# A selective-scan layer with attention beside it: products moved a step later, two engines in source order

## The chip, the cores and the metric

The kernel runs on one core of a Trainium2 chip. The metric is the device time of one execution in microseconds (us); the median of three runs of the kernel before is 5548.85 us (5548.56 to 5548.85). TensorE does the matrix products into PSUM, VectorE and ScalarE do the elementwise work, the scans and the activations, GpSimd a few copies and the indirect transfers, and SyncE (SP) issues nearly all DMAs. Each engine works through its own queue in order; semaphores tie the queues together.

## The reference, cut to what matters

One decoder layer on x of shape (8, 512, 512): a Mamba block, cross-attention with 16 heads over a context of 512 rows, and a mixture of 32 experts with a gate and a shared expert; a layer norm stands after each.

```python
# the Mamba block: D_INNER = 1024, D_STATE = 16
xn = layernorm(x);  x_main, z = split(xn @ in_proj_w)
x_main = silu(causal_depthwise_conv(x_main))          # 4 taps
dt, B_ssm, C_ssm = split(x_main @ x_proj_w)
dt = softplus(dt @ dt_proj_w + dt_proj_b)
# for every time step t, channel d, state n:
h = exp(A * dt) * h + dt * B_ssm * x_main
y = sum_n(h * C_ssm) + x_main * D_param
out = res_scale * ((y * silu(z)) @ out_proj_w) + residual
# then
x = layernorm(x + out)
x = layernorm(x + cross_attention(x, ctx))
x = layernorm(x + experts(x))
```

## The kernel before

All data are float32. The function `layers` holds the Mamba block, the attention, the gate and the shared expert; `experts` and `finish` come after it. The span has three parts: the scan loop up to about 3700 us, the attention of the last batch alone up to about 3945 us, and the experts and the last layer norm.

**The scan loop.** The eight batches are cut into chunks of T = 256 time steps, two per batch (t = 0 and 1), so 16 chunks. A chunk has 32 steps k, one for each pair of channel blocks q (4), group of four states g (4) and channel block ci (2); 512 steps in all. A step scans four states of 128 channels at once. Its pieces:

- `carry` (L448): takes a buffer h (four exist) and ScalarE copies the state from the chunk before into its column 0 (L452).
- `decays` (L442): ScalarE computes exp(A·dt) into one of two buffers l_da, four activations (L446). It is called one step ahead, for step k+1.
- `scan` (L455): VectorE multiplies dt·x by the broadcast B (L458), runs the scan over 1028 columns (L462) and, in a first chunk, saves the state (L464).
- `collect` (L466): VectorE multiplies h by the broadcast C (L479); TensorE adds the states up into the PSUM tile py with four products by a constant matrix (L483), and for g = 0 puts D·x under them with two more (L471).
- `gated` (L491): after eight steps VectorE multiplies the gate z by py (L495). There is one py.
- `bcast` (L380): DMAs that spread B and C of the next group over the partitions, six buffers bc.

**Work beside the scans.** At fixed steps the loop also calls `back` (the output projection of the chunk before, L512, and its layer norm), `gate_x` (z, L311 and L357), `prepare` (softplus of dt for the next q: L398 on TensorE, L408 to L414 on ScalarE, L418 to L421 on VectorE, then the DMAs into `both`), `norm_x`, `flip_x`, `convolve` (L311, L331, L337 and the taps L345) and `x_proj` for the next chunk. A list `side` holds the attention, gate and shared expert of the batch before, cut into units with a weight: `maximum` (L775 on TensorE, L777 on VectorE), `weigh` (L801, exponential L805 on ScalarE), `gather` (L817), dense products (L712) and others. The function `work` gives the weight of each step's own TensorE work, and units are taken as long as the weights keep pace.

**How consumers are placed.** A unit returns a closure that holds the work of the next engine. `do` runs a unit, then lets every closure that is waiting take one stage (`settle`), then appends the new one; `dry` runs `settle` until nothing is left.

**What sets the order.** Every engine's queue is made by the scheduler: it plays the program through with a cost model and issues what is ready, by priority. Source order is only the priority, except for the instructions pinned with `keep_in_program_order`. PSUM tiles that are shared: two of tag mm (dense products, projections), two of tag sc (ps_s and ps_t), one py, one po.

Of the kernel before, what the change touches and what calls it, by code (L numbers as in the profile page):

```python
# [8 lines left out]
F32 = mybir.dt.float32  # L9
# [3 lines left out]
ALU = mybir.AluOpType  # L13
# [4 lines left out]
P = 128  # L18
# [6 lines left out]
NST = 16  # L25
RANK = 32
CC = DI // P
T = 256
NT_ = T // P
NG = 4  # L30
HP = P // 2
# [51 lines left out]
def layers(ctx, tc, a, x1d, filld, based, xbuf):  # L83
# [23 lines left out]
    nc = tc.nc  # L107
# [11 lines left out]
    psy = ctx.enter_context(tc.tile_pool(name="l_psy", bufs=1, space=PSUM))  # L119
# [322 lines left out]
    def decays(c, g, dt, da):  # L442

        for n in range(NG):
            j, m = n // 2, n % 2
            nc.scalar.activation(da[:, n, 1:], dt[:, c % 2, j, :], AF.Exp, scale=aneg[:, c, j, g, m : m + 1])  # L446

    def carry(t, c, g):  # L448

        last = state[:, c, g].unsqueeze(2)  # L450
        h = mp.tile([P, NG, T + 1], F32, tag="h", name="h", bufs=4)
        nc.scalar.copy(h[:, :, 0:1], last if t else nothing)  # L452
        return h
# [9 lines left out]
        if t < S // T - 1:  # L463
            nc.vector.tensor_copy(state[:, c, g].unsqueeze(2), h[:, :, T : T + 1])  # L464

    def collect(c, g, h, bc, py, f):  # L466


        if g == 0:
            for j in range(2):  # L470
                nc.tensor.matmul(  # L471
                    py[j * HP : (j + 1) * HP, c % 2, :],
                    ident[:, j * HP : (j + 1) * HP],
                    f["xs"][c // 2][:, c % 2, :],
                    start=(c % 2 == 0),
                    stop=False,
                )
        steps = h.rearrange("p (j m) t -> p j m t", j=2)[:, :, :, 1:]
        nc.vector.tensor_tensor(steps, steps, bc[1], ALU.mult)  # L479
        for m in range(NG // 2):  # L480
            for j in range(2):
                s = (g, m, c % 2)
                nc.tensor.matmul(  # L483
                    py[j * HP : (j + 1) * HP, c % 2, :],
                    twice,
                    h[:, j * 2 + m, 1:],
                    start=False,
                    stop=(s == (NST // NG - 1, NG // 2 - 1, 1)),
                )

    def gated(q, f, py):  # L491

        f["xs"].pop(q)
        pair = f["zs"][:, 2 * q : 2 * q + 2, :]
        nc.vector.tensor_tensor(pair, pair, py, ALU.mult)  # L495
# [518 lines left out]
    def do(fn, *args, first=False):  # L1014

        if first:
            dry()
        rest = fn(*args)
        settle()
        if rest:  # L1020
            left.append(rest)

    def work(k):

        front = 6.9 if k in (1, 2) else 3.4 if 3 <= k < 7 or k in (12, 15, 18, 21, 24) else 1.0 if k in (11, 26) else 0.0
        return 1.2 + front

    f = {"xt": x0}
# [12 lines left out]
    bc, n = bcast(f, 0), 0  # L1041
    nc.scalar.activation(aneg, aneg, AF.Exp)
    nc.vector.tensor_scalar(aneg, aneg, -1.0, None, ALU.mult)
    decays(0, 0, f["ready", 0][0], das[0])
    old, side, cleared = None, [], 0

    for i, (b, t) in enumerate(chunks):
        nf = {}
        after = chunks[i + 1] if i + 1 < len(chunks) else None
        if t == 0:  # L1050
            side, spent = units(b - 1) if b else sources(0), 0.0

            own = [work(k) for k in range(len(steps))] * 2
            whole = sum(own) + sum(x[0] for x in side)
        py = None
        for k, (q, g, ci) in enumerate(steps):
            if ci == 0:
                if (q, g) != (CC // 2 - 1, NST // NG - 1):
                    bcn = bcast(f, (g + 1) % (NST // NG))
                else:  # L1060
                    bcn = bcast(nf, 0) if after else None
            h = carry(t, 2 * q + ci, g)

            if k + 1 < len(steps) or after:
                nq, ng, ni = steps[(k + 1) % len(steps)]
                decays(2 * nq + ni, ng, (f if k + 1 < len(steps) else nf)["ready", nq][0], das[(n + 1) % 2])
            scan(t, 2 * q + ci, g, f["ready", q][1], bc, das[n % 2], h)
            n += 1
            if k % 8 == 0:
                if k:  # L1070
                    gated(q - 1, f, py)
                elif old:
                    gated(CC // 2 - 1, old[2], old[3])
                py = psy.tile([P, 2, T], F32, tag="py", name="py")
            if i == 0 and k == 0:
                load("Wo")
            if i == 0 and k == 2:
                biases()
            if k == 0 and old:
                twice_x(*old[:3])  # L1080
# [12 lines left out]
            if after:  # L1093
                if k == 5:
                    load_x(*after, nf)
                if k == 9:
                    norm_x(nf)
                if k == 11:
                    for j in range(DC // 2):
                        do(flip_x, j, nf)  # L1100
                if k in (12, 15, 18, 21):
                    do(convolve, after[1], (k - 12) // 3, nf, first=(k == 12))
                if k == 23:
                    dry()
# [19 lines left out]
        old = (b, t, f, py)  # L1124
        f = nf
    gated(CC // 2 - 1, old[2], old[3])
    twice_x(*old[:3])
    for j in range(2):
        do(back, j, *old[:3], first=True)
    dry()  # L1130
    for _, fn, alone in units(B - 1):
        do(fn, first=alone)
# [347 lines left out]
```

## Time and profile before

| | us |
|---|---|
| median of three runs | 5548.85 |
| the profiled execution | 5555.79 |
| its span, first to last instruction | 5554.1 |
| TensorE busy | 4883.9 |
| VectorE busy | 4349.2 |
| ScalarE busy | 2592.8 |
| scans L462: 512 of 2291 ns | 1169.4 |
| products with B and C, L458 and L479 | 617.5 and 621.9 |
| decays L446: 2048 of 499 ns | 888.7 |

The page is one execution on the chip. Busy time of TensorE is modelled: matmuls are pipelined, and the tail of each group counts. "Idle before" is time in which an engine stood still ahead of an instruction, put down to the engine that ended it. Forty equal slices of the span, in tenths of busy time, show that VectorE is nearly full for two thirds of the span and TensorE in the rest:

```profile
PE   6768889888988988888888898879899999999994
DVE  7998989989889989899989999864466565555554
ACT  5554565655556555555555655523222222222223
```

### The profile page before, as it was taken

The page shows a single profiled execution, that of the slowest core. Times are in us where ns is not written, and L with a number is a line of the kernel's source. Part 1 is how long each engine was busy: PE and PEld are TensorE (multiplying, and loading weights), DVE is VectorE, ACT ScalarE, POOL GpSimd, SP SyncE. Part 2 cuts the span into 40 slices and gives each one's busy share as a digit, 9 for nine tenths or more (in the row PEclk, how much of TensorE's full clock was granted, in tenths as well). Part 3 has the DMA queues.
Part 4 walks back from the last instruction along what each step waited for, and adds up shares of the span by engine and source line. Part 5 has one row for each costly group of instructions (what it writes and reads, how often), then busy time and mean ns, then how long its engine had stood idle before and what let it go on. Part 6 is the DMA issues. An engine that isn't in the chain of part 4 may idle for free. (4 is left out here: it accounts for less than half of the span.)

```text
span 5554.1 us, 60352 instructions
## 1 busy us (share of the span) xinstructions
PE 4883.9 (88%) x19752; PEld 2720.5 (49%) x19752; DVE 4349.2 (78%) x5738; ACT 2592.8 (47%) x5483; POOL 560.9 (10%) x424
## 2 busy tenths in 40 slices
PE   6768889888988988888888898879899999999994
PEld 3334344334434434443443343333577777777773
DVE  7998989989889989899989999864466565555554
ACT  5554565655556555555555655523222222222223
POOL 1000002002000200200010020010111111111111
PEclk7878999999999999999999999989999999999997
DMA  6887345445534634544463464441345444454444
GB/s 183 246 239 203 108 130 184 114 120 154 167 104 113 203 92 129 184 123 113 124 199 104 114 193 110 113 157 44 102 121 125 125 125 124 121 126 124 115 121 146
DMA packets 554282, 769.83 MB, mean 139 GB/s; under 512 B 135754, under 2 KB 268394, under 8 KB 551920
## 3 DMA queue, kind: packets, MB, share of 16 engines
q1 hardware_dynamic: 517952, 677.55, 41.5%
q0 software_dynamic: 33280, 76.90, 7.3%
q10 hardware_dynamic: 2736, 11.54, 0.5%
q8 instruction: 156, 2.56, 0.2%
q14 instruction: 158, 1.29, 0.1%
HBM read 508.68 MB, written 165.05 MB: 121 GB/s over the span
## 5 line engine op out<-in xcount | busy, mean ns | idle before, releaser
L446 ACT ACTIVATE l_da<-both,l_aneg 128x256 f32<-128x256 f32 x2048 | 888.7, 499 | 791.5 <-DVE h L462 744.2
L462 DVE TENSOR_TENSOR_SCAN h<-l_da,h 128x1028 f32<-128x1028 f32 x512 | 1169.4, 2291 | 49.9 <-ACT h L452 27.3
L483 PE MATMUL py<-h,l_twice 128*64 128x256 f32 x4096 | 632.0, 424 | 194.2 <-DVE h L479 194.0
L458 DVE TENSOR_TENSOR h<-both,bc 128x1024 f32<-128x1024 f32 x512 | 617.5, 1213 | 141.8 <-PE py L483 78.2
L479 DVE TENSOR_TENSOR h<-h,bc 128x1024 f32<-128x1024 f32 x512 | 621.9, 1218 | 6.3 <-DMA l_qa<-l_ka 0.3
L483 PEld LDWEIGHTS py<-h,l_twice 128*64 128x64 f32 x4096 | 295.2, 148 | 570.5 <-issue 246.4
L775 PE MATMUL ps_s<-l_ka,l_qa 64*128 64x512 f32 x1024 | 315.2, 695 | 141.9 <-DVE mx L777 141.4
L1230 PE MATMUL ps_h<-xT,w 128*128 128x320 f32 x1536 | 435.6, 433 | 0.0
L1310 POOL DMA_INDIRECT based<-y,xe x160 | 251.2, 1570 | 1313.4 <-ACT y L1333 573.4
L1251 DVE TENSOR_TENSOR hT<-ps_h,p 128x320 f32<-128x320 f32 x128 | 62.9, 491 | 379.1 <-PE ps_h L1230 379.1
L777 DVE TENSOR_REDUCE mx<-ps_s 128x2 f32<-128x1024 f32 x256 | 310.2, 1215 | 56.2 <-PE ps_s L775 55.5
L1230 PEld LDWEIGHTS ps_h<-xT,w 128*128 128x128 f32 x1536 | 292.2, 190 | 118.2 <-issue 0.4
L801 PE MATMUL ps_t<-l_qa,l_ka 64*128 64x512 f32 x1024 | 300.6, 651 | 15.0 <-ACT eT L805 11.4
L805 ACT ACTIVATE eT<-ps_t 128x1024 f32<-128x1024 f32 x256 | 258.7, 1012 | 109.2 <-PE ps_t L801 108.7
L817 PE MATMUL po<-eT,l_va 128*64 128x512 f32 x1024 | 281.5, 628 | 24.6 <-ACT raw L829 20.8
L650 POOL DMA_INDIRECT xbuf<-x2t,dest x128 | 218.7, 1708 | 815.8 <-DVE dest L644 777.4
L1230 PE MATMUL ps_h<-t,s 128*128 128x320 f32 x1024 | 286.1, 432 | 0.0
L712 PE MATMUL ps_p<-x2T,wa 128*128 128x512 f32 x512 | 247.5, 633 | 11.8 <-DVE hT L892 10.3
L311 PE MATMUL ps_z<-xnT,wm 128*128 128x256 f32 x1024 | 241.0, 389 | 17.8 <-DVE o L521 17.0
L311 PE MATMUL ps_x<-xnT,wm 128*128 128x256 f32 x1024 | 242.5, 390 | 2.9 <-DMA wm<-in_in_proj_w 2.0
L512 PE MATMUL po<-wm,zs 128*128 128x512 f32 x512 | 234.6, 608 | 3.9 <-DMA wm<-in_out_proj_w 1.8
L1230 PEld LDWEIGHTS ps_h<-t,s 128*128 128x128 f32 x1024 | 194.6, 190 | 81.1
(234 smaller groups left out, 7414.6 us busy)
## 6 DMA issues: line engine op xcount, KB each, us to landing
bc<-scr SPq DMA_DIRECT2D x1024, 128.0 KB
w<-in_w SPq DMA_DIRECT2D x93, 1024.0 KB
wm<-in_in_proj_w SPq DMA_DIRECT2D x128, 512.0 KB
xbuf<-zero SPq DMA_DIRECT2D x32, 1362.5 KB
xe<-xbuf SPq DMA_DIRECT2D x32, 1362.5 KB
both<-dt SPq DMA_DIRECT2D x256, 128.0 KB
both<-dtx SPq DMA_DIRECT2D x256, 128.0 KB
wm<-in_out_proj_w SPq DMA_DIRECT2D x64, 512.0 KB
```

What stands on the lines that cost most here:

```text
L311: nc.tensor.matmul(ps[:, i, :], w[:, dc, i * P : (i + 1) * P], f["xnT"][:, dc, :], start=(dc == 0), stop=(dc == DC - 1),)
L446: nc.scalar.activation(da[:, n, 1:], dt[:, c % 2, j, :], AF.Exp, scale=aneg[:, c, j, g, m : m + 1])
L458: nc.vector.tensor_tensor(steps, dtx[:, c % 2].unsqueeze(2).to_broadcast([P, 2, NG // 2, T]), bc[0], ALU.mult)
L462: nc.vector.tensor_tensor_scan(flat, da.rearrange("p n t -> p (n t)"), flat, 0.0, ALU.mult, ALU.add)
L479: nc.vector.tensor_tensor(steps, steps, bc[1], ALU.mult)
L483: nc.tensor.matmul(py[j * HP : (j + 1) * HP, c % 2, :], twice, h[:, j * 2 + m, 1:], start=False, stop=(s == (NST // NG - 1, NG // 2 - 1, 1)),)
L775: nc.tensor.matmul(ps[:, j, :], qa[r, lt * P : (lt + 1) * P], ka[r, :], start=True, stop=True)
L777: return lambda: nc.vector.tensor_reduce(mx[:, lt, :].unsqueeze(2), ps, AX.X, ALU.max) and None
L801: nc.tensor.matmul(ps[:, j, :], ka[r, kc * P : (kc + 1) * P], qa[r, :], start=True, stop=True)
L805: nc.scalar.activation(eT, ps, AF.Exp)
L817: nc.tensor.matmul(po[j * 2 * HD : (j + 1) * 2 * HD, :], va[:, kc, i, j * HD : (j + 2) * HD], eT[:, j, :], start=(kc == 0), stop=(kc == SC ...
L1230: nc.tensor.matmul(ps, w[:, n, r * P : (r + 1) * P], x[:, n, :], start=not more and n == 0, stop=n == 1, skip_group_check=more,)
```

## The change

Four things change, all in `layers` and its call:

1. `collect` keeps the product with C on VectorE, but returns its TensorE products as a closure, which the loop calls at the end of the next step, ahead of that step's own `collect`. py is now taken inside that closure and kept in `f`; `gated` moves from steps 0, 8, 16, 24 to 1, 9, 17, 25.
2. `carry` is called one step ahead, beside `decays`.
3. `settle` is called right behind the scan, and again only by the units of the step; the call ahead of `collect` is gone. `back`, `gate_x` and silu of z come one step later (2 and 3, 4 to 7, 8), and `work` and the condition for side units follow them.
4. The scheduler no longer orders TensorE and VectorE inside `layers`: both take the source's order. ScalarE, GpSimd and SP are still ordered by the scheduler, with the other two given.

```diff
-    def collect(c, g, h, bc, py, f):
-        if g == 0:
-            for j in range(2):
-                nc.tensor.matmul(
-                    py[j * HP : (j + 1) * HP, c % 2, :],
-                    ident[:, j * HP : (j + 1) * HP],
-                    f["xs"][c // 2][:, c % 2, :],
-                    start=(c % 2 == 0),
-                    stop=False,
-                )
+    def collect(c, g, h, bc, f):
         steps = h.rearrange("p (j m) t -> p j m t", j=2)[:, :, :, 1:]
         nc.vector.tensor_tensor(steps, steps, bc[1], ALU.mult)
-        for m in range(NG // 2):
...
+        xs = f["xs"][c // 2]
+        def products():
+            if g == 0 and c % 2 == 0:
+                f["py"] = psy.tile([P, 2, T], F32, tag="py", name="py")
+            py = f["py"]
+            if g == 0:
...
+            for m in range(NG // 2):
...
+        return products
-    def gated(q, f, py):
+    def gated(q, f):
...
-        front = 6.9 if k in (1, 2) else 3.4 if 3 <= k < 7 or k in (12, 15, 18, 21, 24) else 1.0 if k in (11, 26) else 0.0
+        front = 6.9 if k in (2, 3) else 3.4 if 4 <= k < 8 or k in (12, 15, 18, 21, 24) else 1.0 if k in (11, 26) else 0.0
...
+    ahead, products = carry(0, 0, 0), None
...
-            h = carry(t, 2 * q + ci, g)
+            h = ahead
             if k + 1 < len(steps) or after:
                 nq, ng, ni = steps[(k + 1) % len(steps)]
+                ahead = carry(t if k + 1 < len(steps) else after[1], 2 * nq + ni, ng)
                 decays(...)
             scan(t, 2 * q + ci, g, f["ready", q][1], bc, das[n % 2], h)
-            if k % 8 == 0:
-                if k:
-                    gated(q - 1, f, py)
+            if k % 8 == 1:
+                if k > 1:
+                    gated(q - 1, f)
                 elif old:
-                    gated(CC // 2 - 1, old[2], old[3])
-                py = psy.tile([P, 2, T], F32, tag="py", name="py")
+                    gated(CC // 2 - 1, old[2])
...
-            if k in (1, 2) and old:
-                do(back, k - 1, *old[:3], first=True)
-            if 3 <= k < 7:
-                do(gate_x, k - 3, f, first=(k == 3))
-            if k == 7:
+            settle()
+            if k in (2, 3) and old:
+                do(back, k - 2, *old, first=True)
+            if 4 <= k < 8:
+                do(gate_x, k - 4, f, first=(k == 4))
+            if k == 8:
                 dry()
                 silu(f["zs"])
...
-            if side and (k >= 3 or t and k == 0):
+            if side and (k >= 4 or t and k < 2):
...
-            settle()
-            collect(2 * q + ci, g, h, bc, py, f)
+            if products:
+                products()
+            products = collect(2 * q + ci, g, h, bc, f)
...
+    products()
+    gated(CC // 2 - 1, old[2])
...
         with ExitStack() as ctx:
+            ctx.enter_context(tc.manual_schedule(engines={mybir.EngineType.DVE, mybir.EngineType.PE}))
             layers(ctx, tc, a, x1d, filld, based, xbuf)
```

More of the change, by code (lines that the diff above doesn't have):

```diff
@@ L464, in scan @@
             nc.vector.tensor_copy(state[:, c, g].unsqueeze(2), h[:, :, T : T + 1])
-    def collect(c, g, h, bc, py, f):
-        if g == 0:
-            for j in range(2):
-                nc.tensor.matmul(
-                    py[j * HP : (j + 1) * HP, c % 2, :],
-                    ident[:, j * HP : (j + 1) * HP],
-                    f["xs"][c // 2][:, c % 2, :],
-                    start=(c % 2 == 0),
-                    stop=False,
-                )
+    def collect(c, g, h, bc, f):
         steps = h.rearrange("p (j m) t -> p j m t", j=2)[:, :, :, 1:]
         nc.vector.tensor_tensor(steps, steps, bc[1], ALU.mult)
-        for m in range(NG // 2):
[L481 to L489, printed above, removed]
-    def gated(q, f, py):
+        xs = f["xs"][c // 2]
[4 more added lines that the diff above has]
+            if g == 0:
+                for j in range(2):
+                    nc.tensor.matmul(
+                        py[j * HP : (j + 1) * HP, c % 2, :],
+                        ident[:, j * HP : (j + 1) * HP],
+                        xs[:, c % 2, :],
+                        start=(c % 2 == 0),
+                        stop=False,
+                    )
+            for m in range(NG // 2):
+                for j in range(2):
+                    s = (g, m, c % 2)
+                    nc.tensor.matmul(
+                        py[j * HP : (j + 1) * HP, c % 2, :],
+                        twice,
+                        h[:, j * 2 + m, 1:],
+                        start=False,
+                        stop=(s == (NST // NG - 1, NG // 2 - 1, 1)),
+                    )
+        return products
+    def gated(q, f):
         f["xs"].pop(q)
         pair = f["zs"][:, 2 * q : 2 * q + 2, :]
-        nc.vector.tensor_tensor(pair, pair, py, ALU.mult)
+        nc.vector.tensor_tensor(pair, pair, f["py"], ALU.mult)
     def twice_x(b, t, f):
@@ L1054, in layers @@
             whole = sum(own) + sum(x[0] for x in side)
-        py = None
         for k, (q, g, ci) in enumerate(steps):
@@ L1079, in layers @@
             if k == 0 and old:
-                twice_x(*old[:3])
-            if k in (1, 2) and old:
-                do(back, k - 1, *old[:3], first=True)
-            if 3 <= k < 7:
-                do(gate_x, k - 3, f, first=(k == 3))
-            if k == 7:
+                twice_x(*old)
+            settle()
[4 more added lines that the diff above has]
+            if k == 8:
                 dry()
@@ L1123, in layers @@
             do(fn, first=alone)
-        old = (b, t, f, py)
+        old = (b, t, f)
         f = nf
-    gated(CC // 2 - 1, old[2], old[3])
-    twice_x(*old[:3])
+    products()
+    gated(CC // 2 - 1, old[2])
+    twice_x(*old)
     for j in range(2):
-        do(back, j, *old[:3], first=True)
+        do(back, j, *old, first=True)
     dry()
```

## The prediction

> **What bounds the kernel now.** I read the windows view first, to see which engine has no room, then the waits of that engine, then its timeline, to see what a wait and a step without a wait cost. Three stretches: the scan loop with everything beside it (70 to 3700 us), the last batch's attention alone (to 3945), the experts (to 5554).
>
> ```profile
> 70.00:3700.00 3630.00, 3093.65 (x12640) 1472.95 (x12640) 3293.36 (x3782) 2039.82 (x4346) 272.76 (x197) 0.92 0.51 147
> 3945.00:5554.00 1609.00, 1535.90 (x6272) 1133.85 (x6270) 925.95 (x1724) 452.68 (x978) 251.22 (x160) 0.98 0.48 122
> ```
>
> The columns are the stretch, its length, busy us of TensorE, its weight load, VectorE, ScalarE and GpSimd, then clock, DMA share and GB/s. In the scan loop VectorE is busy 3293 of 3630 us; only 337 us are left to win there. TensorE's 3094 us are less than they look: eight records of py last 1.08 us as a group, but the next group starts 0.92 us after them (2009.17 to 2010.09), so the tail of each group is counted as busy. The experts are TensorE's and lie outside the changed functions. So the question is what VectorE waits for in the loop, before and after. Its waits between 70 and 3700 us, the longest:
>
> ```profile
> DVE h L458 <- PE py L483: 78.2, 33, 5.2
> DVE h L458 <- DMA both<-dtx: 43.8, 20, 6.9
> DVE xs L345 <- ACT xs L337: 29.7, 21, 2.8
> DVE h L462 <- ACT h L452: 27.3, 15, 2.0
> DVE zs L495 <- PE py L483: 23.9, 17, 2.4
> DVE m L60 <- ACT r L58: 7.6, 15, 0.5
> DVE dtx L418 <- ACT dtx L414: 5.7, 1, 5.7
> ```
>
> (us in total, times, longest.) All rows of that answer add up to 297 us. The first, fourth and fifth are the change's target: the products come so late on TensorE that buffers of h, and py, are not free. Two stretches of VectorE's timeline (start, length, instruction, idle before) hold the other two prices:
>
> ```profile
> 3659.69 0.18 DVE L583 TENSOR_SCALAR g_rank<-g_rank 128x32 f32<-128x32 f32 x1
> 3659.91 0.29 DVE L584 TENSOR_TENSOR g_work<-g_work,g_rank 128x128 f32<-128x128 f32 x1
> 3660.23 0.29 DVE L589 TENSOR_REDUCE g_w<-g_work 128x4 f32<-128x128 f32 x1
> ...
> 3661.21 0.28 DVE L596 TENSOR_REDUCE g_m<-g_oh 128x4 f32<-128x128 f32 x1
> 3661.41 0.68 DVE L892 TENSOR_TENSOR hT<-hT,ps_p 128x512 f32<-128x512 f32 x1
> ...
> 2539.93 1.22 DVE L777 TENSOR_REDUCE mx<-ps_s 128x2 f32<-128x1024 f32 x1
> 2542.38 1.22 DVE L777 TENSOR_REDUCE mx<-ps_s 128x2 f32<-128x1024 f32 x1 [1.23 <-PE ps_s L775]
> 2543.52 0.68 DVE L495 TENSOR_TENSOR zs<-zs,py 128x512 f32<-128x512 f32 x1
> 2544.11 1.22 DVE L458 TENSOR_TENSOR h<-both,bc 128x1024 f32<-128x1024 f32 x1
> 2545.43 2.30 DVE L462 TENSOR_TENSOR_SCAN h<-l_da,h 128x1028 f32<-128x1028 f32 x1
> ```
>
> An instruction that reads what the one right before it wrote starts 0.03 to 0.04 us after that one's end (L584, L589); one that doesn't starts 0.08 us before it (L892, L495). The scan right behind its own L458 starts 0.10 us after it, so that pair costs 0.18 more than an independent one. And two maxima next to each other cost 1.23 us of idle time.
>
> **What the Trainium skill says.** "PSUM — Partial Sum Buffer", section "Engine vs sequencer instructions": "ScalarE/VectorE/GpSimdE queues are strict FIFO." The trace agrees: ScalarE's decays wait up to 5.3 us for a scan with other work behind them. So whatever stands behind a waiting decay waits too. "VectorE: DVE Perf Modes", section "The DRAIN you can't avoid", says that the next operation does not start until the pipe is empty and that a semaphore costs nothing extra; the trace differs, as shown: the wait on the neighbour costs 0.11 to 0.18 us. "ScalarE: Activation LUTs", section "What ACT_TABLE_LOAD costs", has 1283 ns and a drain of about as much again; the trace has 1.28 us and no drain (load at 2004.95, next instruction at 2006.24). "Perfetto Trace Analysis", section "Optimization Strategy" of its performance part, reads a repeated gap as a missing buffer; the 1.23 us between two maxima is that, with two buffers for ps_s and ps_t together.
>
> **The change part by part.** I work in us against the profiled execution (5555.8, span 5554.1); the median of the runs is 5548.9, so I take 6.9 off at the end. Lines are those of before; the statements are the same after. Counts are of the order in which the built instructions stand.
>
> 1. Waits removed: with TensorE's products in the source's place, one step late, py frees h in time: the carry for a step asks for products two steps old. The whole 297 goes, and what waits afterwards is put back below. −297.
>
> 2. VectorE in source order loses its interleaving. Before, the scheduler put a foreign instruction between dependent ones; after, every step is L458, L462, L464, consumers, L479. Instructions in the loop that wait for their direct predecessor: 847 before, 2155 after. L458 to L462: 146 to 512, 366 × 0.17 = 62. The taps L345: 42 to 256, 214 × 0.06 = 13 (six taps together last 2.71 us, so their gap is nearer −0.02). The other 728 (L464, dt, layer norms, the gate's chain of small operations): × 0.11 = 80. Together +155. Bounds 100 and 180.
>
> 3. ScalarE's order puts consumers behind decays that VectorE itself must release. The decays for step k+2 wait for scan k, because there are two l_da; in after's ScalarE queue they stand ahead of work for which VectorE waits right after scan k. Worked example, step 11 of a first chunk: VectorE runs scan, L464, L697, L418. L418 needs L414, and the queue before L414 is: four decays (released by this scan), L452, L408, L409, L408, L409, L410, L300, L412, L414. From this view of ScalarE:
>
> ```profile
> 2022.88 1.71 ACT L446 ACTIVATE l_da<-both,l_aneg 128x256 f32<-128x256 f32 x4 [3.16 <-DVE h L462]
> 2034.83 0.64 ACT L410 ACTIVATE u<-u 128x512 f32<-128x512 f32 x1
> 2036.25 0.65 ACT L412 ACTIVATE l<-u 128x512 f32<-128x512 f32 x1
> 2036.77 0.65 ACT L414 ACTIVATE dtx<-u 128x512 f32<-128x512 f32 x1
> ```
>
> 1.62 + 0.10 + 1.44 (four at 0.36) + 0.64 + 0.50 + 0.60 + 0.60 = 5.5, less L464 and L697 on VectorE (0.85): 4.6 us idle. The same subtraction at each place of a batch (its two chunks): first chunk: step 3 (layer norm, L60) 1.4; step 9 (silu with two table loads ahead of L495 and L60) 2.6; 11: 4.6; 16 and 18 (L345 behind L337) 3.4 and 1.5; 27 (L418 again, with an eT in between) 4.6. Second chunk: 3: 1.6; 9: 0.7; 11: 4.1; 16: 2.7; 20: 0.5; 22 (L345, the gate's exp) 3.7. Sum 31.4 × 7 batches = 220, and 10 in the first, which has no attention beside it: +230. These are floors where the durations hold, since the queue can't be passed; but stalls elsewhere in the same step would be counted twice, so bounds 130 and 260.
>
> 4. Two L777 stand side by side where the second's matmul needs the buffer that the first frees, at five steps of a batch (20, 25, 30 and 0, 10): 5 × 1.3 × 7, and 0.2 in the ramp: +48.
>
> 5. Left-over waits for DMAs (xt, xr, bc, both) and for TensorE: both<-dt now starts three to four steps before its use, so 44 of the old wait should go. SP keeps its scheduled order: its bc loads stand behind wm loads that wait for TensorE, in both kernels. I take +30; bounds 10 and 110.
>
> 6. The end: before, TensorE still had ps_p (L712) to do after the last L479 (3684.3) and ended L512 at 3716.9, 32.6 later. After, the side work is in the steps; py 0.9, then 16 matmuls of 0.48: some 10. −22, and about 8 us of the gate's work on VectorE moves ahead of the last step: −14 together.
>
> 7. At no price: carry a step earlier (four h, three alive), xs a step longer (five buffers), py allocated a step later (gated reads it before the first product writes), the shifted hooks back, gate_x, silu; VectorE's work covers them. If TensorE fell two steps behind, L458 would wait as before (78).
>
> Sum: −297 + 155 + 230 + 48 + 30 − 14 = +152; 5708 for the profiled execution, 5701 for the median: 5700.
>
> **Rivals.**
> - Faster: ScalarE's stalls don't come, because its other waits leave the consumers done early. Parts 2 and 6 leave 297 − 155 + 14 = 156 us: the sum of VectorE's waits in the loop decides, below 156 it is faster. With 48 + 30 + 40 = 118 it is 5549 − 38 = 5511. For it: before, the same subtraction finds more waits for ScalarE than the trace has (some 115 against 91). Against: part 3's queue is fixed. 0.09.
> - No change: half of the ScalarE stalls are swallowed and the pairs cost 110: −297 + 110 + 135 + 40 + 25 − 14 = −1, so 5548. 0.05.
> - Slower still: TensorE in source order blocks on slots of mm, ps_s and xr and is the late one, and SP's bc loads behind it; part 5 at 110 and more: 5780 to 5850. For it: before, TensorE waited 141 us for L777. Against: VectorE's pace leaves it room, since the tails of its groups are counted as busy (above). 0.13.
> - The forecast, 5600 to 5780: 0.73.
>
> **How the numbers follow.** Low ends: −297 + 100 + 170 + 45 + 30 − 14 = +34, so 5583; I take 5590. High ends: −297 + 180 + 260 + 50 + 70 − 14 = +249, so 5800. Left out: faster 0.09, same 0.05, above 5800 0.06. A measurement tells 0.2% (11 us) from no change. Faster 0.09, same 0.05, slower 0.86.
>
> **What would show it.** Right: in VectorE's waits after, L458 <- py near zero; L418 <- L414 near 95 us, L345 <- L337 near 70, L60 and L495 <- ScalarE near 50, L777 <- ps_s near 48; VectorE's timeline with L462 0.10 behind L458 in every step; the last scan near 3860. Wrong: VectorE's waits in the loop below 156 us, or L458 <- py still in front, or the loop's length unchanged.

## The result, and the profile after

The changed kernel takes 5959.26 us (median of four runs, 5954.69 to 5960.71) against 5548.85: a ratio of 1.0736, 95% interval 1.0717 to 1.0755. It is slower, by 259 us more than the forecast of 5700, and lies above the forecast's range of 5600 to 5780.

The three parts of the span, in the windows view of the kernel after (loop and experts; columns as before):

```profile
70.00:4095.00 4025.00, 3184.41 (x12692) 1506.84 (x12692) 3410.32 (x3789) 1989.37 (x4308) 196.86 (x200) 0.88 0.46 133
4344.00:5953.00 1609.00, 1535.15 (x6272) 1133.96 (x6271) 926.04 (x1724) 452.67 (x978) 252.83 (x160) 0.98 0.48 122
```

The experts take the same 1609 us. From here on "the loop" runs from 70 us to the last product with C (L479 of before, L469 of after). Before it was 3613 us with VectorE busy 3284; after it is 4025 us with 3410. The attention of the last batch alone, between the loop and the experts, is 13 us shorter. So 412 us come in the loop, and 126 of them are a VectorE that is busy longer with the same work. VectorE's waits of the kernel after in the loop, the longest (total, times, longest, us):

```profile
DVE xs L345 <- ACT xs L337: 116.6, 32, 9.9
DVE o L529 <- PE po L520: 104.4, 30, 8.4
DVE dtx L418 <- ACT dtx L414: 92.7, 22, 5.2
DVE mx L785 <- PE ps_s L783: 55.2, 51, 1.7
DVE m L60 <- ACT r L58: 40.6, 37, 1.9
DVE total L856 <- ACT r L855: 29.0, 7, 7.7
DVE zs L503 <- ACT zs L362: 29.0, 8, 3.8
...
DVE h L458 <- PE py L489: 1.6, 1, 1.6
```

The waits for h, first in the list before, are down to 1.6 us, and VectorE waits for no DMA any more. But all rows together make 521 us where they made 290 in the same stretch: 310 end with ScalarE, 209 with TensorE. (Line numbers after are those of before plus 8 between the product with C and the end of the loop: L529, L785 and L503 are L521, L777 and L495 of the prediction; L469 and L489 are L479 and L483.) The pair that prices the lost interleaving, in VectorE's timeline after:

```profile
4062.50 1.22 DVE L469 TENSOR_TENSOR h<-h,bc 128x1024 f32<-128x1024 f32 x1
4063.64 1.22 DVE L458 TENSOR_TENSOR h<-both,bc 128x1024 f32<-128x1024 f32 x1
4064.96 2.30 DVE L462 TENSOR_TENSOR_SCAN h<-l_da,h 128x1028 f32<-128x1028 f32 x1
4067.18 0.66 DVE L900 TENSOR_TENSOR hT<-hT,ps_p 128x512 f32<-128x512 f32 x1
```

L458 starts 0.08 before its neighbour ends, the scan behind its own L458 0.10 after it. The forty slices of the page after:

```profile
PE   5658878887887888788788878878999999999995
DVE  6897888888888888888888888886445556665554
ACT  4454554554455455445545544552322222222223
```

VectorE, at 8 and 9 tenths before, is at 8 nearly throughout the loop, and TensorE at 7 and 8: no engine is full there any more.

One wait stands for what the prediction did not have. VectorE and TensorE of the kernel after, at steps 1 to 3 of a chunk (start, length, instruction, idle before it and what is put down as its end):

```profile
2034.00 0.68 DVE L503 TENSOR_TENSOR zs<-zs,py 128x512 f32<-128x512 f32 x1
...
2042.05 2.30 DVE L462 TENSOR_TENSOR_SCAN h<-l_da,h 128x1028 f32<-128x1028 f32 x1
2044.39 0.17 DVE L464 COPY l_state<-h 128x4 f32<-128x4 f32 x1
2051.75 0.75 DVE L529 SCALAR_TENSOR_TENSOR o<-po,l_rs,o 128x512 f32<-128x512 f32 x1 [7.19 <-PE po L520]
```

```profile
2034.83 1.12 PE L479 MATMUL py<-xs,l_ident 128*64 128x256 f32 x4 [8.94 <-ACT l_da L446]
2035.70 1.95 PE L489 MATMUL py<-h,l_twice 128*64 128x256 f32 x8
2037.58 7.33 PE L520 MATMUL po<-wm,zs 128*128 128x512 f32 x16
2044.85 0.65 PE L479 MATMUL py<-xs,l_ident 128*64 128x256 f32 x4
2045.33 1.03 PE L489 MATMUL py<-h,l_twice 128*64 128x256 f32 x8
2046.29 7.13 PE L520 MATMUL po<-wm,zs 128*128 128x512 f32 x16
```

TensorE stands still for 8.94 us. The view puts the end of this wait down to ScalarE's L446; but L479 uses nothing of L446's, while VectorE has just read py (L503 ends at 2034.68), and there is one py, which L479 writes. So py is what TensorE waits for. Only then can the output projection follow, which also reads the zs that L503 writes: 7.33 and 7.13 us in its two halves. VectorE comes to L529 two steps later, 9.9 us after the end of L503, and waits for the rest. A half is eight matmuls, two records each, so one costs 0.90 us and not the 0.48 that the prediction used. The trace of the kernel before had nearly the same price, 0.87 in the last projection:

```profile
3701.09 10.46 PE L512 MATMUL po<-wm,zs 128*128 128x512 f32 x24
```

L529 is also issued in the very step of the second half, since the unit `prepare` of step 3 lets the waiting closures take a stage.

### The profile page after: what moved, and what is told of

The parts are those of the page before. It is cut to its first block, busy times and chain, and to the rows that moved or that the text cites. A ratio compares the mean times of both kernels' runs of the same rounds, so it can differ in the third digit from the quotient of the medians.

```text
span 5952.9 us, 60265 instructions
## 1 busy us (share of the span) xinstructions
PE 4952.0 (83%) x19752; PEld 2741.6 (46%) x19752; DVE 4465.5 (75%) x5738; ACT 2537.3 (43%) x5433; POOL 483.9 (8%) x424
## 5 line engine op out<-in xcount | busy, mean ns | idle before, releaser
L446 ACT ACTIVATE l_da<-both,l_aneg 128x256 f32<-128x256 f32 x2048 | 890.9, 499 | 1166.3 <-DVE h L462 1151.3
L489 PE MATMUL py<-h,l_twice 128*64 128x256 f32 x4096 | 616.7, 425 | 147.8 <-DVE h L469 147.3
L458 DVE TENSOR_TENSOR h<-both,bc 128x1024 f32<-128x1024 f32 x512 | 623.5, 1218 | 9.5 <-DMA bc<-scr 7.9
L469 DVE TENSOR_TENSOR h<-h,bc 128x1024 f32<-128x1024 f32 x512 | 624.1, 1219 | 5.7
L489 PEld LDWEIGHTS py<-h,l_twice 128*64 128x64 f32 x4096 | 288.3, 148 | 510.7 <-issue 187.7
L783 PE MATMUL ps_s<-l_ka,l_qa 64*128 64x512 f32 x1024 | 309.7, 685 | 104.2 <-DVE mx L785 80.2
L785 DVE TENSOR_REDUCE mx<-ps_s 128x2 f32<-128x1024 f32 x256 | 310.1, 1217 | 101.8 <-PE ps_s L783 101.2
L720 PE MATMUL ps_p<-x2T,wa 128*128 128x512 f32 x512 | 281.9, 706 | 16.1 <-DVE hT L900 8.4
L345 DVE SCALAR_TENSOR_TENSOR xs<-xp,l_cw,xs 128x256 f32<-128x256 f32 x384 | 180.1, 483 | 139.5 <-ACT xs L337 130.4
L658 POOL DMA_INDIRECT xbuf<-x2t,dest x128 | 180.6, 1411 | 893.8 <-DVE dest L652 354.9
L311 PE MATMUL ps_z<-xnT,wm 128*128 128x256 f32 x1024 | 246.7, 396 | 4.6 <-DMA wm<-in_in_proj_w 4.6
L311 PE MATMUL ps_x<-xnT,wm 128*128 128x256 f32 x1024 | 244.7, 393 | 0.5 <-ACT xnT L300 0.5
L520 PE MATMUL po<-wm,zs 128*128 128x512 f32 x512 | 232.5, 607 | 0.8 <-DMA wm<-in_out_proj_w 0.8
```

The lines of the kernel that those rows point to most:

```text
L311: nc.tensor.matmul(ps[:, i, :], w[:, dc, i * P : (i + 1) * P], f["xnT"][:, dc, :], start=(dc == 0), stop=(dc == DC - 1),)
L458: nc.vector.tensor_tensor(steps, dtx[:, c % 2].unsqueeze(2).to_broadcast([P, 2, NG // 2, T]), bc[0], ALU.mult)
L489: nc.tensor.matmul(py[j * HP : (j + 1) * HP, c % 2, :], twice, h[:, j * 2 + m, 1:], start=False, stop=(s == (NST // NG - 1, NG // 2 - 1, 1)),)
L720: nc.tensor.matmul(ps, lhs(dc), rhs(dc), start=(dc == 0), stop=(dc == DC - 1))
L783: nc.tensor.matmul(ps[:, j, :], qa[r, lt * P : (lt + 1) * P], ka[r, :], start=True, stop=True)
L785: return lambda: nc.vector.tensor_reduce(mx[:, lt, :].unsqueeze(2), ps, AX.X, ALU.max) and None
```

## The experiments

All times are medians; ratios are to the kernel before on the same chip, with 95% intervals. The kernel before took 5551 to 5558 us beside them, so differences of some 10 us between times that were not taken together say nothing. The table splits VectorE's loop of the main runs: busy, waits by the engine that ended them, and the rest (the loop less both), which is the small gaps behind neighbours. "Source order" is the order in which the program states the instructions; "by scheduler" leaves it to the scheduler. L458 ahead of L469 is experiment 4, the others follow in the text.

| kernel | time | loop | busy | waits TensorE / ScalarE / DMA | rest |
|---|---|---|---|---|---|
| before | 5549 | 3613 | 3284 | 131 / 91 / 68 | 38 |
| changed | 5959 | 4025 | 3410 | 209 / 310 / 0 | 94 |
| moves, all by scheduler | 5608 | 3675 | 3302 | 165 / 114 / 48 | 46 |
| moves, TensorE in source order | 5779 | 3847 | 3309 | 335 / 115 / 43 | 45 |
| moves, VectorE in source order | 5861 | 3933 | 3408 | 153 / 277 / 0 | 95 |
| no moves, both in source order | 6485 | 4556 | 3430 | 575 / 446 / 14 | 91 |
| changed, L458 ahead of L469 | 5920 | 3985 | 3351 | 246 / 332 / 4 | 52 |
| changed, back at 1 and 2 | 5889 | 3955 | 3410 | 138 / 311 / 0 | 95 |
| changed, dt on VectorE later | 5947 | 4015 | 3413 | 265 / 240 / 0 | 96 |
| changed, dense halved | 5881 | 3959 | 3407 | 181 / 276 / 0 | 94 |

**1. Moves or order: four kernels.** The two halves of the change apart, and the two engines apart. The line that puts both engines into source order:

```diff
             ctx.enter_context(tc.manual_schedule(engines={mybir.EngineType.DVE, mybir.EngineType.PE}))
```

The line left out of the changed kernel:

> The changed kernel with all its moves (products with C a step later, carry ahead, consumers behind the next scan), but with all five engines ordered by the scheduler again. Theory (the source's order costs the time: lost interleaving on VectorE, ScalarE's queue, TensorE blocked in its queue): the moves are harmless, 5500 to 5600 us; VectorE's waits in the loop 200 to 330 us, o L529 <- po below 20, its busy time in the loop back near 3300. Rival (the moves themselves cost it, whoever orders): above 5800 us, L529 and L345 still with some 100 us each.

The line put into the kernel before:

> The kernel before with nothing moved, TensorE and VectorE in the source's order. Theory (the order costs): as slow as the changed kernel or slower, 5900 to 6150 us, since the products stand in the same step and the h and py waits that the moves take away are added to the lost interleaving; L458 <- py above 60 us. Rival (the moves cost it): near 5550 us, at most 5650.

The changed kernel with PE (TensorE) alone in the line:

> The changed kernel with TensorE alone in the source's order; VectorE by the scheduler. If VectorE's own order is most of the loss (lost overlap some 180 us, and ScalarE's late results met by a queue that can't be passed, some 310 us), 5600 to 5720 us: VectorE's busy time in the loop near 3300, L345 and L418 below half of 117 and 93. If TensorE blocking in its queue is most of it (rival), 5800 us or more, with o L529 <- po still near 100 us.

With DVE (VectorE) alone:

> The changed kernel with VectorE alone in the source's order; TensorE by the scheduler. If VectorE's own order is most of the loss, 5800 to 5900 us: only the waits for TensorE shrink (209 us in the loop: L529 104, the maxima 55, and so on, to about 80). If TensorE blocking in its queue is most of it (rival), below 5700 us. If neither alone is most of it, both kernels with one engine in source order lie between 5650 and 5850.

Measured: the moves with all engines by the scheduler 5607.88 us, ratio 1.0091 (1.0074 to 1.0108); the order without the moves 6485.44, 1.1666 (1.1646 to 1.1685); TensorE alone 5779.26, 1.0398 (1.0378 to 1.0418); VectorE alone 5860.94, 1.0546 (1.0528 to 1.0563).

So the order costs the time: of the 410 us the moves alone bring some 50, VectorE's order 253 on top (5608 to 5861), and TensorE's order 171 alone or 98 beside VectorE's. The table says in what. With VectorE in source order its busy time grows by 106 and the rest by 48, and the waits that end with ScalarE from 114 to 277. With TensorE in source order under a scheduled VectorE, only the waits for TensorE grow, from 165 to 335. The row of VectorE's waits for L458 in the run with the moves alone, and then with TensorE's order added:

```profile
DVE h L458 <- PE py L489: 111.6, 73, 5.7
```

```profile
DVE h L458 <- PE py L489: 267.2, 95, 13.6
```

The wait for h, which the moves were expected to take away, is larger with them than without (78.2). What takes it away is VectorE's own order: with VectorE in the source's order it is at most 33 us in every run. In the kernel before with both in source order it is not on VectorE either, but on ScalarE, whose carry copies into the same buffer; ScalarE's waits there:

```profile
ACT h L452 <- PE py L483: 1060.5, 344, 13.9
ACT l_da L446 <- DVE h L462: 765.2, 424, 9.9
```

In the changed kernel:

```profile
ACT h L452 <- PE py L489: 313.5, 193, 7.2
```

So in source order the moves are worth 526 us (6485 to 5959). Probably it is because ScalarE's queue no longer stands so long at L452; no run took the moves apart, so that is not shown. The expected numbers of this run (5900 to 6150, L458 above 60) missed that; those of VectorE alone held for the time, but its waits for TensorE fell only to 153 and not to 80; those of TensorE alone held for VectorE's busy time and for L345 (28; L418 has no row), but its time lies between the two theories, and it is L458 that waits and not L529 (4). The moves alone came out 8 us above the first theory's 5600.

**2. ScalarE in source order too.**

```diff
-            ...engines={mybir.EngineType.DVE, mybir.EngineType.PE}))
+            ...engines={mybir.EngineType.DVE, mybir.EngineType.PE, mybir.EngineType.Activation}))
```

> The changed kernel with ScalarE in the source's order as well. If it is the scheduler's order on ScalarE that puts L414 and L337 too far back (part 3 of the prediction), VectorE's waits for ScalarE fall from 310 us to below 200 and the time to 5820 to 5900 us; L418 <- L414 below 50. Rival (any fixed order on ScalarE puts them behind decays that the scan releases, since the source has the decays of the next step first): waits for ScalarE 300 us or more, the time 5940 to 6050.

5965.86 us, 1.0742 (1.0724 to 1.0760): no change. The time is the rival's, but neither expectation describes the waits: those for ScalarE fell, from 310 to 233 us, and those for TensorE rose by as much, from 209 to 284. This was the first sign that waits in this kernel don't add up.

**3. The output projection one step earlier.**

```diff
-        front = 6.9 if k in (2, 3) else ...
+        front = 6.9 if k in (1, 2) else ...
-            if k in (2, 3) and old:
-                do(back, k - 2, *old, first=True)
+            if k in (1, 2) and old:
+                do(back, k - 1, *old, first=True)
-            if side and (k >= 4 or t and k < 2):
+            if side and (k >= 4 or t and k < 1):
```

> The changed kernel with the output projection (back) called at steps 1 and 2 again, as before, instead of 2 and 3; nothing else moved. If L529's 104 us of waiting come from TensorE's price for that projection (16 matmuls of 0.87 us, where the prediction had 0.48) and from the one step that lies between, L529 <- po falls to 0 to 30 us and the time by 60 to 100: 5860 to 5900 us. Rival (TensorE is late whatever stands there): the wait moves to the next consumer of TensorE, time within 30 us of 5959.

5888.94 us, 1.0600 (1.0582 to 1.0617): 70 us, as the first theory has it. The L529 wait fell from 104 to 20:

```profile
DVE o L529 <- PE po L520: 19.5, 12, 5.7
```

In its timeline the projection's second half ends before VectorE comes:

```profile
2007.37 7.13 PE L520 MATMUL po<-wm,zs 128*128 128x512 f32 x16
```

```profile
2015.57 1.40 DVE L529 SCALAR_TENSOR_TENSOR o<-po,l_rs,o 128x512 f32<-128x512 f32 x2
```

**4. The lost overlap.** The product with B of the next step ahead of the product with C of this one:

```diff
-    def scan(t, c, g, dtx, bc, da, h):
+    def feed(c, dtx, bc, h):
...
+    def scan(t, c, g, da, h):
...
+            if k + 1 < len(steps) or after:
+                feed(2 * nq + ni, ..., bcn if ci else bc, ahead)
             products = collect(2 * q + ci, g, h, bc, f)
```

> The changed kernel with the next step's product with B (L458) issued ahead of this step's product with C (L469), so that no scan stands right behind its own L458 and fewer L469 right behind their scan. If the lost interleaving on VectorE (0.18 us for each of 512 pairs, as the timeline has it) is time on the path, 90 to 120 us go: 5840 to 5870. Rival (VectorE is paced by ScalarE's and TensorE's results, so that a shorter step only waits longer): less than 40 us go, and the waits of VectorE grow from 521 us by 60 or more.

5920.29 us, 1.0657 (1.0639 to 1.0675). Busy time fell by 59 and the rest by 42: 101 us, 0.20 for each of 512 pairs where the timeline says 0.18. But the waits grew from 521 to 582, and only 39 us came off, as the rival has it. The price of the pair is right (the 101 us also hold some L469 that no longer stand right behind their scan); its worth on the path is 40% of it.

**5. dt on VectorE a step later.** To take away the L418 wait:

```diff
+            if k % 8 == 4 and dts:
+                left.append(dts()())
...
-                    do(prepare, q + 1, f)
+                    dts = prepare(q + 1, f)()
```

> The changed kernel with the four VectorE instructions of dt (L418 to L421) issued right behind the next step's scan instead of behind the scan of the step that starts dt; its ScalarE part stays. If part 3 is right that VectorE stands still for L414 behind four decays (21 times 4.0 to 4.5 us, 93 in all), that wait falls below 15 us and the time by 70 to 100: 5860 to 5890 us. Rival (the three engines are tied to each other, so that a wait taken away comes back at the next consumer): less than 40 us go, VectorE's waits in the loop stay above 480 of 521 us.

5947.25 us, 1.0699 (1.0682 to 1.0717). The edit does one thing more than its heading says: without `do` at steps 3, 11, 19 and 27, the waiting closures are not let go on there, so L529 moves from step 3 to step 4. The wait at L418 is down from 93 to 1.4 us and that at L529 from 104 to 32, but the time fell by only 12 us (some 20 by the ratios). In their place stand, with 55 and no row at all in the changed kernel:

```profile
DVE mx L785 <- PE ps_s L783: 129.3, 76, 5.2
DVE k L705 <- PE ps_p L720: 42.6, 7, 6.9
```

84 us of these are new waits at the steps of the old L418 wait or one behind (L785 at 11 of second chunks and 27 of first ones, L705 at 12); another 34 are L785 at steps 19, 20 and 30 of first chunks. Step 11 of a second chunk shows how. VectorE in the changed kernel:

```profile
2365.11 2.30 DVE L462 TENSOR_TENSOR_SCAN h<-l_da,h 128x1028 f32<-128x1028 f32 x1
2371.45 0.69 DVE L418 SCALAR_TENSOR_TENSOR dtx<-dtx,u 128x512 f32<-128x512 f32 x1 [4.04 <-ACT dtx L414]
...
2374.23 1.22 DVE L785 TENSOR_REDUCE mx<-ps_s 128x2 f32<-128x1024 f32 x1
```

The same step with dt moved, VectorE:

```profile
2361.50 2.30 DVE L462 TENSOR_TENSOR_SCAN h<-l_da,h 128x1028 f32<-128x1028 f32 x1
2369.02 1.22 DVE L785 TENSOR_REDUCE mx<-ps_s 128x2 f32<-128x1024 f32 x1 [5.22 <-PE ps_s L783]
```

and there TensorE and ScalarE:

```profile
2361.69 1.12 PE L398 MATMUL ps_dt<-xd,l_w_dt 32*128 32x256 f32 x4
2362.75 0.66 PE L295 MATMUL ps_t<-l_ident,xt 128*128 128x128 f32 x4
2365.85 1.12 PE L295 MATMUL ps_t<-l_ident,xt 128*128 128x128 f32 x4 [2.45 <-ACT dt L409]
2366.90 2.08 PE L783 MATMUL ps_s<-l_ka,l_qa 64*128 64x512 f32 x4
```

```profile
2363.84 0.51 ACT L446 ACTIVATE l_da<-both,l_aneg 128x256 f32<-128x256 f32 x1 [1.83 <-DVE h L462]
...
2365.32 0.48 ACT L409 ACTIVATE dt<-ps_dt,l_b_dt 128x256 f32<-128x256 f32 x1
```

The scan frees l_da; the decay goes; L409 reads dt's product and so frees its PSUM buffer of tag mm; only then can the second group of transposes L295 go, and behind it, in TensorE's source order, the scores L783 for which VectorE's L785 waits. L418 and L785 hang on the same burst of ScalarE. With L418 in front, its wait covered the other (L785 came at once at 2374.23); without it, L785 waits 5.22 itself, and the 2.8 us of L418 to L421 still have to be done, one step later. In the changed kernel L785 began 9.1 us after its scan did, here 7.5.

**6. That PSUM buffer freed.** In the same kernel dt's TensorE and ScalarE part at steps 10 and 26 instead of 11 and 27:

```diff
-            if k % 8 == 3:
+            if k in (3, 10, 19, 26):
```

> The changed kernel with dt's VectorE part a step later (5947 us), and with dt's TensorE and ScalarE part one step earlier at steps 10 and 26 of a chunk (11 and 27 before), where the layer norm's transposes L295 or the next products waited for its slot of mm. If the slot is the second chain behind the L418 wait, TensorE's wait L295 <- ACT dt L409 (32 us) falls below 8, the waits L705 <- ps_p and those of mx at these steps (85 us together) go, and the time falls by 60 to 90: 5855 to 5890 us; both dt repairs together are then worth what the L418 wait was, 93. Rival (a third chain is as late): less than 25 us go, 5920 or more.

5945.04 us, 1.0699 (1.0681 to 1.0717): no change against experiment 5, as the rival has it. L295 no longer waits for L409; the dense product L720 at the step before does, 25 us, and VectorE's L705 waits there instead (27 us at step 10 where it had 43 at step 12). The buffer was still scarce, one step earlier.

**7. Repairs together.** Back at 1 and 2, L458 ahead of L469 and dt later; then with TensorE by the scheduler; then the three with the edit of 6:

> Three repairs at once: the output projection at steps 1 and 2, the next step's product with B ahead of this step's product with C, dt's VectorE part a step later. Alone the first took 70 us and the second 39 us (101 us of lost overlap gone, 61 back as waits). If each is a cost of its own, they add up with the third to 200 to 270 us: 5690 to 5760. Rival (shared slack: what one frees another takes): less than 150 us, 5810 or more.

> The same three repairs with VectorE alone in the source's order, TensorE by the scheduler (5861 us without the repairs). If what the second repair frees on VectorE is then not taken by a blocked TensorE, the step is worth its 100 us here and L418 its 69, the projection little: 5680 to 5720. Rival (VectorE's order still meets late results): 5760 or more.

> All four repairs (5885 us with three). If the slot held back the others too, 60 to 100 us go: 5785 to 5825. Rival: 5860 or more.

Three: 5884.67 us, 1.0586 (1.0568 to 1.0603), 75 us where the parts alone gave 70 + 39 + 12. Three with TensorE by the scheduler: 5720.56, 1.0291 (1.0274 to 1.0308), 140 us off that kernel's 5861, at the edge of the first theory's numbers. Four: 5841.76, 1.0513 (1.0496 to 1.0531), another 43 us off the three, between its two expectations; the same fourth edit had given nothing without the other two. So repairs neither add up nor keep their worth: three together gave less than their sum, the fourth gave more than alone. With TensorE in source order too, three repairs are worth about half of what they are under the scheduler (75 against 140 us).

**8. Less work for TensorE.** These kernels leave out half of each dense product, so their output is another: the changed kernel, the same with dt later, with three repairs, and the kernel before:

```diff
-        for dc in range(DC):
-            nc.tensor.matmul(ps, lhs(dc), rhs(dc), start=(dc == 0), stop=(dc == DC - 1))
+        for dc in range(DC // 2):
+            nc.tensor.matmul(ps, lhs(dc), rhs(dc), start=(dc == 0), stop=(dc == DC // 2 - 1))
```

> The changed kernel with half of the contraction of every dense product of the attention, the gate and the shared expert left out (two of four matmuls at L720; the output is another); VectorE and ScalarE have the same instructions. It takes some 408 matmuls of 0.87 us, 355 us of TensorE's work, out of the loop, and at most 35 us out of the tail. If TensorE is the late one, the time falls by 150 to 250 us: 5710 to 5810. Rival (VectorE and ScalarE set the pace): by less than 80, the tail included: 5880 or more.

> The same cut, and dt's VectorE part a step later, which took off 12 us with the whole products. If TensorE was what stood behind the L418 wait, the repair is now worth 60 to 100 us more than the cut alone. Rival: again 0 to 25 us.

> The same cut and all three repairs, which took off 75 us with the whole products. If TensorE was the late one, the overlap (101 us) and L418 (93 us) now count: 150 to 230 us below the cut alone. Rival: 60 to 90 us.

> Control: the kernel before with the same cut. Its VectorE is busy 91% of the loop and waits 131 us for TensorE, so the cut gives little: 30 to 100 us, tail included, 5450 to 5525. If it gives as much as in the changed kernel, TensorE is late in both and the source's order is not what made it so.

5880.74 us (1.0591, 1.0574 to 1.0609), 5862.90 (1.0555, 1.0538 to 1.0573), 5804.99 (1.0452, 1.0434 to 1.0469) and, before, 5410.25 (0.9743, 0.9726 to 0.9759). The rivals came true, and in the kernel before the cut gave more than its expected 30 to 100 us. In the changed kernel TensorE's busy time in the loop falls by 290 us and the loop by 66; in the kernel before, by 300 and 140. (The granted clock of the loop fell in both by 0.03, so that does not set them apart.) The repairs are worth 18 and 76 us on top, as with the whole products. L529 and L418 in the changed kernel, with the cut:

```profile
DVE o L529 <- PE po L520: 105.3, 30, 8.5
DVE dtx L418 <- ACT dtx L414: 93.3, 23, 5.0
```

They are what they were. For L529 this says little, since no dense product is called at steps 2 and 3 and TensorE had stood still for 8.94 us before the projection anyway. For L418 it says that TensorE's backlog is not behind the wait: it starts at a fixed place in ScalarE's queue and takes its own length. The scheduled kernel turns 47% of the freed TensorE time into a shorter loop, the one in source order 23%.

**9. A faster kernel.** Two scheduled versions: the moves with five buffers of h (and five bc), and the kernel before with dt a step earlier.

```diff
-    bcp = ctx.enter_context(tc.tile_pool(name="l_bc", bufs=6))
+    bcp = ctx.enter_context(tc.tile_pool(name="l_bc", bufs=5))
-        h = mp.tile([P, NG, T + 1], F32, tag="h", name="h", bufs=4)
+        h = mp.tile([P, NG, T + 1], F32, tag="h", name="h", bufs=5)
```

> All engines by the scheduler with the change's moves (the first experiment, 5608 us), with five buffers of h instead of four, and five bc instead of six to make room. If its L458 <- py (112 us, more than the 78 of the kernel before) is what makes it slower than the kernel before, that wait falls below 20 us and the time to 5490 to 5540, faster than the kernel before. Rival (TensorE is the late one, and the wait turns up at other consumers, or bc becomes late): 5570 to 5620 us, with L458 <- bc or the waits for TensorE grown by 60 us.

```diff
-            if k % 8 == 3:
+            if k % 8 == 2:
```

> The kernel before, all engines by the scheduler, with dt prepared one step earlier (steps 2, 10, 18, 26 instead of 3, 11, 19, 27). Its waits L458 <- DMA both<-dtx, 44 us, should go, and nothing else change: 5500 to 5530 us, faster than both kernels. Rival (the scheduler places dt by its priorities anyway, and five h buffers showed that L458 then waits for another thing): 5545 to 5570.

5604.57 us, 1.0090 (1.0073 to 1.0107), and 5554.71, 0.9991 (0.9981 to 1.0001). In the first, L458 <- py fell from 112 to 85 and L458 <- DMA both rose from 34 to 123; in the second L458 <- DMA both stayed at 39. Neither beats the kernel before.

## Why the prediction was wrong, by its steps

The sum for the loop was +166 (−297 + 155 + 230 + 48 + 30); the loop grew by 412. Of the miss of 246, 124 lie in the term for left-over waits (5), and 32 more at a place of term 3 whose chain also comes through TensorE.

1. *Waits removed, −297.* The waits are gone (290 in this stretch), but not by the cause given, so that the size fits is luck. "py frees h in time" is not what the moves do: with VectorE under the scheduler that wait is longer with the moves than without, 112 us, and 267 with TensorE in source order as the argument has it. VectorE's own order removes it; why is not shown.
2. *Lost interleaving, +155.* Right: VectorE's order alone adds 106 + 48 = 154 with TensorE scheduled; from before to after it is 126 + 55 = 181, of which 17 + 8 come with the moves already. But experiment 4 gave back only 39 of 101 us when the pairs were taken apart.
3. *ScalarE's order, +230.* Right in its mechanism, and at most of its places to a few tenths: L418 waits 4.5 us at step 11 of a first chunk, 4.4 at 27 and 4.0 at 11 of a second chunk (forecast 4.6, 4.6 and 4.1), L345 mostly 3.4 to 3.8 and 1.6 at 16 and 18, and 2.7 at 16 of a second chunk (3.4, 1.5 and 2.7). In sum it is 310, because three places were missed. L856 at step 16 of a second chunk, 29 us in all, is not among the waits that were named; step 9 of a first chunk took 4.7 and not 2.6 (15 in all); and step 22 of a second chunk 8.4 to 9.9, six times, 58 in all, where 3.7 (26 in all) stood for another reason. There the chain comes through TensorE:

```profile
1931.02 1.97 PE L886 MATMUL ps_tr<-l_ident,x2t 128*128 128x128 f32 x8 [13.74 <-ACT x2t L80]
1944.17 3.72 PE L311 MATMUL ps_x<-xnT,wm 128*128 128x256 f32 x16
1947.92 0.59 ACT L331 COPY xp<-ps_x 128x512 f32<-128x512 f32 x1 [3.44 <-PE ps_x L311]
1949.24 2.96 DVE L345 SCALAR_TENSOR_TENSOR xs<-xp,l_cw,xs 128x256 f32<-128x256 f32 x6 [9.79 <-ACT xs L337]
```

   TensorE stands 13.74 us at L886 for x2t, which ScalarE's L80 makes after a layer norm on VectorE (L74 to L78, done at 1930.1); L311, for which L345 waits through ScalarE, stands behind it in TensorE's source order.
4. *Pairs of maxima, +48.* Right: 55, 48 of it at the five steps that were named (the term's own product comes to 46).
5. *Left-over waits for DMAs and TensorE, +30, bounds 10 and 110: the step that failed.* DMAs gave nothing. TensorE gave 209 − 55 = 154, 124 more than the 30, and with the 32 at step 22 that came through it 156. The other 90 of the 246 us missed are the rest of ScalarE's order (48), overlap (26), maxima (7), the waits of before (7) and VectorE behind itself (2). Even with 110 in this term the forecast's high end would have been 5838. L529 alone, 104, was nearly nothing in the forecast. Two errors stand behind it. The projection was priced at 0.48 us a matmul where the trace before has 0.87. At 0.48 its two halves would have taken some 6.8 us less than their 14.5, nearly the whole of the 7.2 + 1.0 that VectorE waits in the chunk shown (an estimate from the rows above). And the argument against the last rival, "VectorE's pace leaves it room", judged TensorE by its load. In source order TensorE stands at the first instruction that is not ready, for VectorE 510 and for ScalarE 310 us of the loop, and chains that cross engines begin late. But TensorE's order is not all of it: under the scheduler, with VectorE alone in source order, VectorE still waits 153 us for TensorE (maxima 79, L529 52).
6. *The end, −14.* 13, but not by its parts: after the last product with C TensorE took 16 us for py and the projection, not some 10, by the same wrong price.
7. *At no price.* `back` a step later was not free. Moved back, it is worth 70 us.

The rival "slower still" came nearest: TensorE does block in source order. But what it stood for ahead of L529 and of the longest L345 was py and x2t, not the slots that the rival named; VectorE waited for no bc load, and its 5780 to 5850 were too low. The median was also 5 us above the profiled execution, not 7 below it.

What stays open: which chain sets the pace over the whole loop. The first three repairs gave back less than the waits and gaps that they removed, the projection's 70 of 84, the others far less, and other waits grew; where they stand was followed at a few steps alone, and no one chain was found for the rest. Nor is it separated what TensorE's clock adds: with the same work TensorE was busy 106 us longer in the loop, at a granted clock of 0.88 instead of 0.92.

## What to carry to other kernels

When queues lose their freedom, the waits at a place can be forecast from the order of the queues, here to a few tenths of a us at most places; but a wait is not a cost that can be taken away alone: ask what is the second-latest thing at the same place, and whether it hangs on the same release. An engine below its full load is no cover in a fixed order; what counts is where its chain starts and how long it is, priced from that very line's own records. In this kernel starting a chain earlier (`back`: 70 us off for 84 us of wait) paid; putting consumers later (dt, and with it L529: 12 us off for 91 + 72) did not.

## What the runs showed of the hardware

- A product of 128 rows with 512 columns in float32 cost 0.90 us on TensorE (L520: sixteen records, two for each matmul, in 7.13 to 7.33).
- In these runs the granted TensorE clock went with TensorE's busy share of the loop, not against it: 0.92 at 85% (before), 0.88 at 79% (changed), 0.85 at 73% (changed, dense products halved) and 0.85 at 74% (no moves, source order). The experts had 0.98 at 95%. Why is not shown.
- Taking L458 away from in front of its own scan freed 101 us of VectorE's time, 0.20 us a step: 59 us as shorter busy time and 42 as smaller gaps.
